# A two-layer block on one core: slots found by matmuls, biases gathered per slot, a reworked opening, and part of the first pass in seven products

## The chip, the core and the metric

The kernel runs on one core of a Trainium2 chip. A core has TensorE (PE), VectorE (DVE), ScalarE (ACT), GpSimd (POOL) and SyncE (SP), which run their own instruction streams and meet at semaphores, and 16 DMA engines. The metric is the device time of one execution in microseconds. The kernel before takes 2854.79 us, the median of three runs (2854.2 to 2859.41).

## The reference

There are 8 x 256 = 2048 tokens of 512 channels, all in float32. The block has two layers, each of the form x + attention(norm(x)) + ffn(norm(x)).

```python
xn = _layernorm(x)
x = x + _L0_attn_ref(xn, ...) + _L0_ffn_ref(xn, ...)
xn = _layernorm(x)
x = x + _L1_attn_ref(xn, ...) + _L1_ffn_ref(xn, ...)
```

Layer 0's attention is a linear attention with 32 heads of 128: q, k, v (with silu) and a gate (sigmoid), each a projection of 512 channels to 4096; scores times a decay instead of a softmax; a root-mean-square norm over all heads; gate times result through an output projection of 4096 to 512. Layer 0's feed-forward is a mixture of 16 experts with two chosen per token, plus a shared expert:

```python
scores = softmax(xt @ router_w + router_b) + router_bias
# keep the best 2 of 4 groups, then the best 2 experts of those
y += ge[:, None] * ((silu(xt @ w1 + b1) * (xt @ w2 + b2)) @ w3 + b3)   # each expert
z = (silu(xt @ sw1 + sb1) * (xt @ sw2 + sb2)) @ sw3 + sb3              # shared
```

Note that the expert's output bias b3 is inside the bracket that the gate multiplies. Layer 1 is one softmax attention head of 128 and a feed-forward of 64 low-rank adapters of rank 16, with 16 chosen per token.

## The kernel before

**Tiling.** Tokens are handled in four chunks of 512 (`NCH`), each of four tiles of 128 (`TPC`). The kernel has four stages.

**1. The opening** (lines 140 to 525). Per chunk: `normalize` (226) on DVE with a root on ACT; `turn_rows` (240), four PE transposes per tile into a bank and one copy out; `token_sums` (369), sums and differences of token blocks on POOL, stored to DRAM (`xc`) for the later passes; `shared_up` (317), the shared expert's up projections, 16 matmuls of 512 columns; `route` (265), router matmuls of 16 columns and then the choice on DVE; `decays` (357), exponentials on ACT; `clear` (410), zeros written over `xd`, a DRAM buffer of 47 x 128 slots; and, one chunk late, `share` (347), which calls `shared_down` (329). That one transposes the gates (L333), copies them, and for each token tile multiplies the 17 gates into the 17 rows of biases (L338) ahead of the shared expert's two products (L340). All expert biases are thus added per token. `first_two` (250) chooses two of n by comparing all pairs, n x n elements a token. Router weights, gates, choices and masks lie in the pool `work1`, whose memory the next stage takes over.

After the last chunk follows the dispatch (447 to 523): two matmuls of counts (L482 to L484), and a chain of small DVE steps that yields, for each token and each of its two choices, a slot in 47 tiles of 128 slots (`slots`, `slot_gates`), each tile owned by one expert (`rows_`).

**2. Attention of layer 0** (599 to 1215), the bulk. It goes over the chunks (pass i), in each over 8 groups of 4 heads (g), in each over the seven products p1 to p7 of a Strassen scheme in Winograd's form (`ORDER` = p1, p2, p6, p5, p3, p7, p4), and each of these is a product of blocks that is itself done in smaller blocks, of 128 channels. An `Outer` (960) is one such step. In passes 2 to 4 the inner blocks too are done in seven products (`p1`, `p7`, `p6`, `p4`, `p2`, `p5` and, inside the following step, `p3`; 1037 to 1066). In the first pass `plain` (981) does them in eight. `product` (661) is four matmuls of 128 columns. `weights` (605) loads a step's four weight blocks; for p6, p5, p3 and p7 it makes them as sums of loaded blocks on DVE (`outer_sum`), and for all makes the four inner sums on POOL (`inner_sum`), which in the first pass only go to DRAM (`ws`) for the later passes. The steps p1, p2 and p4 (`RAW`) have weights that are loaded as they are. Weights lie in a ring of three buffers.

The order of work is written by hand: after each product `slot` (679) takes due pieces from a list that `later(after, f)` (675) fills, "after" being a number of slots; ACT and POOL keep program order here (`manual_schedule`, 599), while the other engines' instructions are ordered by the framework's planner. In SP's queue the DMAs wait in order.

Among the pieces are the experts. In the first pass `row` (1086) loads a tile of normalized tokens from `xnd` and `scatter` (1093) writes its rows to their slots in `xd`, twice, by an indirect DMA on POOL. From the second pass on `Expert` (689) takes the tiles of slots one by one: the tokens from `xd` by SP, the weights by an indirect DMA on POOL, `turn` at 8 slots, `up` at 11, `down` at 14, whose result ACT copies (L733) and SP stores in `yd`. At a pass's end `load_sum` (933) loads the chunk's running sum (`xr`), and `finish` (586) adds the attention to it on DVE.

**3. The hand-over** (`wrapped_up`, 1145): the first chunk's expert results are gathered by slot from `yd` (`gather`, `settle`) and normalized in one piece, with the last steps of attention running.

**4. Layer 1** (1258 on): per chunk a `Head` (routing on 64 columns, q and k on 512, values, softmax) interleaved with the low-rank products in seven. `next_x` (1289) loads the next chunk's sum.

Of the kernel before, what the change touches and what calls it, by code (L numbers as in the profile page):

```python
# [9 lines left out]
FP = mybir.dt.float32  # L10
I32 = mybir.dt.int32
# [6 lines left out]
NT = B * S  # L18
P = 128
# [28 lines left out]
NEVER = -3.0e38  # L48

# [17 lines left out]
def block_kernel(  # L67
# [75 lines left out]
    def once(shape, name):  # L143
        return work.tile(shape, FP, tag=name, name=name, bufs=1)

    scratch = big("scratch").rearrange("p (h b) n -> p h (b n)", h=4)
    xs = [work.tile([P, TPC, C], FP, tag="x", name=f"x{i}", bufs=NCH) for i in range(NCH)]
    x_t = x.rearrange("(i t p) c -> i t p c", t=TPC, p=P)
    for t in range(TPC):
        nc.sync.dma_start(out=xs[0][:, t, :], in_=x_t[0, t])  # L150
# [8 lines left out]
    nc.sync.dma_start(out=wsh, in_=w_sh)  # L159
# [5 lines left out]
    b3_t = held[0 : E + 1, SH * C : (SH + 1) * C]  # L165
    nc.sync.dma_start(out=b3_t, in_=b3)
# [8 lines left out]
    xd = dram.tile([NSLOT, C], FP, name="xd")  # L175
# [7 lines left out]
    xnd = [dram.tile([P, TPC, C], FP, name=f"xnd{i}") for i in range(NCH)]  # L183
# [5 lines left out]
    zero = held[:, (SH + 1) * C : (SH + 2) * C].unsqueeze(1)  # L189
    nc.gpsimd.memset(zero, 0.0)  # L190

    ident = const.tile([P, P], FP, name="ident")
    make_identity(nc, ident)
    eps_t = const.tile([P, 1], FP, name="eps_t")
    nc.gpsimd.memset(eps_t, EPS)
# [5 lines left out]
    before = once([P, E, E], "before")  # L201
# [8 lines left out]
    dist = const.tile([P, S + P], FP, name="dist")  # L210
# [15 lines left out]
    def normalize(o, xc):  # L226

        mv = small.tile([P, TPC, 2], FP, tag="mv", name="mv")
        for t in range(TPC):
            st = small.tile([P, 6], FP, tag="st", name="st")  # L230
            nc.vector.bn_stats(st, xc[:, t, :])
            nc.vector.bn_aggr(mv[:, t, :], st)
        rstd = small.tile([P, TPC], FP, tag="rstd", name="rstd")
        rsqrt(rstd, mv[:, :, 1])
        for t in range(TPC):
            nc.vector.tensor_scalar(
                o[:, t, :], xc[:, t, :], mv[:, t, 0:1], rstd[:, t : t + 1], ALU.subtract, ALU.mult
            )

    def turn_rows(xT, xn, t, pt):  # L240
# [4 lines left out]
        if t % 2:  # L245
            nc.scalar.copy(o, i)
        else:
            nc.vector.tensor_copy(o, i)

# [15 lines left out]
    def route(xT, ge, sel):  # L265

        full = [P, TPC, E]
        pl = ps_sc()
        for t in range(TPC):
            for c in range(NC):  # L270
                mm(
# [57 lines left out]
    def shared_down(i, hT):  # L329
        xc = xs[i]  # L330
        pg = ps_sc()
        for t in range(TPC):
            nc.tensor.transpose(pg[0 : E + 1, bass.ts(t, P)], gates[i][:, t, :], ident)  # L333
# [1288 lines left out]
```

## Time and profile before

| | |
|---|---|
| median of the runs | 2854.79 us |
| the profiled execution, its own time | 2856.16 us |
| its span, first to last instruction | 2854.4 us |
| first projection matmul of the attention (L666) | 164.4 us |
| first matmul of the first p6 step | 186.7 us |
| last matmul of the attention (L878) | about 2551.6 us |
| PE busy / DVE / ACT / POOL | 2796.7 / 1569.7 / 948.2 / 1465.7 us |
| DMA | 763.21 MB, mean 267 GB/s |
| PE idle in passes 2 to 4, 800 to 2550, by releaser | DVE r 7.7, DVE mv 2.6, POOL gT 1.8, others under 1.4 each |

A float32 matmul stands in the trace as two entries (and two weight loads), a transpose as one. The mean length of an entry is longer than what it costs, because entries overlap: what counts is the distance from one start to the next. On a fast clock that is 0.112 us for 128 columns, 0.216 for 256 and 0.43 for 512. POOL's sums of 128x512 take 1.27 us each; an indirect DMA takes POOL 1.0 us to issue, and lands 7.5 us later for the experts' weights (1.3 MB), 7.3 for the scatters and 6.2 for the gathers of 256 KB from `yd` (medians).

### The profile page before, as it was taken

The numbers are of one execution on the slowest core, as the hardware profiler recorded it, in microseconds if no ns is written. First come the engines' busy times: TensorE is split into PE (matmuls) and PEld (weight loads), VectorE is DVE, ScalarE is ACT, GpSimd is POOL, SyncE is SP. The second block draws the span as 40 slices with busy tenths as digits, with TensorE's granted clock in tenths as the row PEclk, the third lists the DMA queues.
The fourth block names the chain that finished last, engine by engine and source line by source line (L and its number), as shares of the span: only waits on it lengthen the run. The fifth ranks groups of instructions, "written<-read, shape, count | busy, mean of one in ns | idle before, by whom it ended". The sixth has DMA issues, their size and how long they took to land. (4 is left out here: it accounts for less than half of the span.)

```text
span 2854.4 us, 49572 instructions
## 1 busy us (share of the span) xinstructions
PE 2796.7 (98%) x19864; PEld 2566.1 (90%) x19864; DVE 1569.7 (55%) x2615; ACT 948.2 (33%) x1683; POOL 1465.7 (51%) x1213
## 2 busy tenths in 40 slices
PE   8989999999999999999999999999999999999999
PEld 4469999999999999999999999999999999987877
DVE  6555666666654445444545555555555555556663
ACT  3312222212244333333443333443444333432221
POOL 4545666665546555555645454545544566552210
PEclk9999999999999999999999999999999999999999
DMA  7888998899986777778877777777777788652211
GB/s 255 301 309 337 357 352 341 341 349 347 364 320 246 262 266 273 282 270 299 296 265 257 264 266 265 259 274 280 284 259 259 267 310 298 222 212 88 76 61 61
DMA packets 161943, 763.21 MB, mean 267 GB/s; under 512 B 18209, under 2 KB 24225, under 8 KB 109874
## 3 DMA queue, kind: packets, MB, share of 16 engines
q1 hardware_dynamic: 149826, 706.25, 66.9%
q0 software_dynamic: 11888, 53.79, 5.2%
q8 instruction: 157, 2.57, 0.4%
q14 instruction: 72, 0.59, 0.1%
HBM read 596.14 MB, written 163.05 MB: 266 GB/s over the span
## 5 line engine op out<-in xcount | busy, mean ns | idle before, releaser
L666 PE MATMUL ps_a<-xt,w 128*128 128x128 f32 x5376 | 750.9, 276 | 11.7 <-DVE r L97 7.7
L666 PEld LDWEIGHTS ps_a<-xt,w 128*128 128x128 f32 x5376 | 681.9, 192 | 30.1 <-issue 14.3
L97 POOL TENSOR_TENSOR c<-c 128x512 f32<-128x512 f32 x216 | 271.7, 1273 | 262.0 <-DVE c L97 259.9
L97 POOL TENSOR_TENSOR c<-c,r 128x512 f32<-128x512 f32 x240 | 318.4, 1347 | 158.9 <-DVE r L97 153.1
L666 PE MATMUL ps_e<-xt,w 128*128 128x128 f32 x2688 | 373.4, 275 | 1.3 <-DVE c L97 1.3
L97 POOL TENSOR_TENSOR sums<-sums,sq 128x512 f32<-128x512 f32 x120 | 153.3, 1278 | 426.4 <-ACT sq L796 425.6
L996 ACT COPY cp<-ps_a 128x512 f32<-128x512 f32 x336 | 196.4, 585 | 476.0 <-PE ps_a L666 468.8
L666 PEld LDWEIGHTS ps_e<-xt,w 128*128 128x128 f32 x2688 | 344.4, 192 | 11.2 <-issue 3.8
L97 POOL TENSOR_TENSOR w<-w 128x512 f32<-128x512 f32 x224 | 294.6, 1325 | 108.2 <-issue 31.2
L666 PE MATMUL ps_a<-w,xt 128*128 128x128 f32 x1792 | 346.7, 275 | 0.0
L858 PE MATMUL ps_sc<-wo,gT 128*128 128x256 f32 x1288 | 305.1, 379 | 1.8 <-POOL gT L97 1.8
L97 DVE TENSOR_TENSOR acc<-ps_sc,acc 128x512 f32<-128x512 f32 x208 | 143.3, 690 | 265.8 <-PE ps_sc L858 198.8
L666 PEld LDWEIGHTS ps_a<-w,xt 128*128 128x128 f32 x1792 | 272.3, 192 | 0.0
L97 DVE TENSOR_TENSOR c<-ps_a,c 128x512 f32<-128x512 f32 x232 | 157.9, 686 | 202.7 <-PE ps_a L666 201.7
L858 PEld LDWEIGHTS ps_sc<-wo,gT 128*128 128x128 f32 x1288 | 232.3, 190 | 26.8 <-POOL gT L97 2.0
L666 PE MATMUL ps_b<-xt,w 128*128 128x128 f32 x1680 | 236.4, 277 | 6.8 <-ACT c L1010 4.2
L801 DVE SCALAR_TENSOR_TENSOR gT<-ps_o,nw,c 128x256 f32<-128x256 f32 x256 | 112.0, 479 | 231.0 <-ACT sq L796 222.0
L666 PEld LDWEIGHTS ps_b<-xt,w 128*128 128x128 f32 x1680 | 217.3, 194 | 17.5 <-issue 8.2
L744 ACT ACTIVATE c<-c 128x512 f32<-128x512 f32 x256 | 148.9, 627 | 170.1 <-DVE c L97 170.0
L796 ACT ACTIVATE sq<-ps_o 128x512 f32<-128x512 f32 x120 | 71.6, 597 | 382.3 <-PE ps_o L782 382.3
L666 PE MATMUL ps_e<-w,xt 128*128 128x128 f32 x896 | 173.2, 275 | 0.0
L97 DVE TENSOR_TENSOR s<-ps_sc,decay 128x384 f32<-128x384 f32 x256 | 139.8, 552 | 40.7 <-PE ps_sc L770 38.1
(299 smaller groups left out, 4635.8 us busy)
## 6 DMA issues: line engine op xcount, KB each, us to landing
w<-in_w_att_dram SPq DMA_DIRECT2D x128, 1024.0 KB
st<-in_w_att_dram SPq DMA_DIRECT2D x32, 1024.0 KB
wo<-in_w_out_dram SPq DMA_DIRECT2D x113, 256.0 KB
decay<-dec SPq DMA_DIRECT2D x64, 384.0 KB
w<-ws0p SPq DMA_DIRECT2D x12, 1792.0 KB
w<-ws1p SPq DMA_DIRECT2D x12, 1792.0 KB
w<-ws2p SPq DMA_DIRECT2D x12, 1792.0 KB
w<-ws3p SPq DMA_DIRECT2D x12, 1792.0 KB
```

The lines of the kernel that those rows point to most:

```text
L97: (eng or nc.vector).tensor_tensor(o, a, b, op)
L666: mm(bank[:, bass.ts(ty, P)], a, b, start=(first and ty == 0), stop=True, skip_group_check=True,)
L744: nc.scalar.activation(qk, qk, AF.Silu)
L796: nc.scalar.activation(sq, po, AF.Square)
L801: nc.vector.scalar_tensor_tensor(gT[:, h, :].rearrange("p (t n) -> p t n", t=2), po[:, bass.ts(h, S)].rearrange("p (t n) -> p t n", t=2), ...
L858: mm(py[:, bass.ts(t, S)], self.O[p][:, hh, bass.ts(t, P)], self.wo[p][:, hh, :], start=(t == 0 and hh == 0), stop=(hh == 1), skip_group_c ...
L996: nc.scalar.copy(c, bank)
```

## The change

- **Tokens.** `xd`, `clear`, `row` and `scatter` go. `find(g)`, once in each group of the first pass, makes for four (choice, tile) pairs a 128x128 matrix of ones where a token's slot has this partition, and a 128x47 one with the token's number where the slot has this tile, and adds up their products on PE: `whose` then holds, for each slot, its token. `Expert` gathers its tokens from `xnd` by an indirect DMA on POOL, next to that of the weights.
- **Biases.** No gates are transposed and no bias matmul stands in `shared_down`. `Expert.bias` gathers for each slot the owner's row of b3 into the token buffer, by a third indirect DMA on POOL at 12 slots, and `down`, now at 18, adds it on DVE in place of ACT's copy. `turn` is at 10, `up` at 13. The shared expert's own bias is broadcast and added by four POOL sums per chunk (`last_bias`).
- **Opening.** Half of the first chunk's tiles are loaded from ACT's queue, and the shared weights too; ACT's root is used once early; 16 transposes of the identity (`WARM`) run on PE ahead of the first data; the first chunk is normalized tile by tile; a chunk's transposes come right after the previous chunk's routing; router matmuls stand between the up projections. `chosen_two` chooses two of 16 with DVE's eight maxima and a replacement; `first_two` stays for the four groups. Gates, choices and masks move from `work1` to the `acc` tile.
- **First pass.** Steps with p in `RAW` (p1, p2, p4) are done in seven inner products in the first pass too; their inner sums, of weights and of tokens, are used on PE at once. The order of the inner sums changes, with 7 first.
- **Hand-over and layer 1.** The first normalization of layer 1 is cut into pieces of the list; the first `Head` interleaves q and k with the routing (`opening`).

```diff
-        nc.sync.dma_start(out=xs[0][:, t, :], in_=x_t[0, t])
+        (nc.scalar if t % 2 else nc.sync).dma_start(out=xs[0][:, t, :], in_=x_t[0, t])
...
+    nc.scalar.activation(root[:, 0:1], eps_t, AF.Sqrt)
+    nc.scalar.dma_start(out=wsh, in_=w_sh)
...
+    idle = ps_o()
+    for n in range(WARM):
+        nc.tensor.transpose(idle[:, bass.ts(n % 4, P)], ident, ident)
...
+    def chosen_two(keep, v):
+        top = scratch[:, 0, 0 : TPC * 8].rearrange("p (t n) -> p t n", t=TPC)
+        rest = scratch[:, 0, TPC * 8 : TPC * (8 + E)].rearrange("p (t n) -> p t n", t=TPC)
+        for t in range(TPC):
+            nc.vector.max(top[:, t, :], v[:, t, :])
+        nc.vector.tensor_copy(pair[:, :, 0:2], top[:, :, 0:2])
+        for t in range(TPC):
+            nc.vector.match_replace(rest[:, t, :], pair[:, t, :], v[:, t, :], -NEVER)
+        nc.vector.tensor_scalar(keep, rest, -NEVER, None, ALU.is_equal)
...
             project(p1, wsh, e, i)
+            between()
             project(p2, wsh, SH + e, i)
+            between()
...
-        gT = work.tile([E + 1, CH], FP, tag="geT", name="geT", bufs=1)
-        nc.scalar.copy(gT, pg[0 : E + 1, :])
         for t in range(TPC):
             py = ps_mm()
-            mm(py, gT[:, bass.ts(t, P)], b3_t, start=True, stop=False)
...
+        pl, tiles = ps_sc(), list(range(TPC))
+        ups.append(shared_up(i, lambda: scores(pl, xT[i], tiles.pop(0))))
+        ge = disp.tile([P, TPC, E], FP, name=f"ge{i}")
+        route(pl, ge, sel_all[:, bass.ts(i, TPC), :])
         gates.append(ge)
+        if i + 1 < NCH:
+            turn(i + 1)
         decays(i)
-        clear(i)
...
+    def last_bias(r, t3):
+        nc.sync.dma_start(out=t3, in_=b3[E : E + 1].to_broadcast([P, C]))
+        for t in range(TPC):
+            add(r[:, t, :], r[:, t, :], t3, nc.gpsimd)
...
-                    if o == 7:
+                    if o == 6:
                         nc.sync.dma_start(out=ws[g][p], in_=w[:, 4 if p in RAW else 1 : 8])
...
+                if p in RAW:
+                    return sums_of(w)
...
+        for t in first_sums:
+            sub(t[:, 4], t[:, 1], t[:, 0], nc.gpsimd)
+            sub(t[:, 1], t[:, 3], t[:, 1], nc.gpsimd)
+            sub(t[:, 5], t[:, 3], t[:, 4], nc.gpsimd)
+            sub(t[:, 6], t[:, 2], t[:, 5], nc.gpsimd)
...
-                nc.sync.dma_start(out=self.xe, in_=xd[bass.ts(j, P), :])
+                nc.gpsimd.indirect_dma_start(
+                    out=self.xe, out_offset=None, in_=xnd[:, :],
+                    in_offset=bass.IndirectOffsetOnAxis(ap=whose[:, j : j + 1], axis=0),
...
+            def bias(self):
+                nc.gpsimd.indirect_dma_start(
+                    out=self.xe, out_offset=None, in_=b3[:, :],
+                    in_offset=bass.IndirectOffsetOnAxis(ap=own_[:, self.j : self.j + 1], axis=0),
...
-                nc.scalar.copy(ye, py)
+                add(ye, py, self.xe)
...
             def go(self, bank, p, first=False):
                 product(bank, self.w[p], self.x[p], first)
                 slot()
+                if self.following:
+                    self.following.step()
...
-            later(8, e.turn)
-            later(11, e.up)
-            later(14, e.down)
+            later(10, e.turn)
+            later(12, e.bias)
+            later(13, e.up)
+            later(18, e.down)
...
+        def find(g):
...
+            for n in range(4):
+                at = 4 * g + n
+                nc.vector.tensor_scalar(ones_[:, n], count_, at_[:, 0, at : at + 1], None, ALU.is_equal)
+                nc.vector.tensor_scalar(
+                    theirs[:, n], count_[:, 0:NMT], at_[:, 1, at : at + 1],
+                    token[:, at % NTT : at % NTT + 1], ALU.is_equal, ALU.mult,
+                )
+            def add_up():
+                pt = ps_sc()
+                for n in range(4):
+                    mm(pt[:, 0:NMT], ones_[:, n], theirs[:, n], start=(n == 0), stop=(n == 3))
...
+            later(3, add_up)
...
+        def sevenfold(n):
+            return plan[n][0] > 0 or plan[n][2] in RAW
...
-            if i == 0:
+            last = outers[n - 1] if n and sevenfold(n - 1) else None
+            if not sevenfold(n):
+                if last:
+                    last.p3()
                 prepare(n + 2)
                 cur.plain(outers[n + 1])
                 continue
+            if i == 0:
+                while cur.steps:
+                    cur.step()
+                cur.following = outers[n + 1]
...
+        def opening(self):
+            self.pf = ps_sc()
...
+                for c in range(NC):
+                    mm(pm, wqkv_t[:, c, bass.ts(n, P)], self.yT[:, c, :], start=(c == 0), stop=(c == NC - 1))
+                    if c % 2:
+                        self.ranks(2 * n + c // 2)
+                nc.scalar.activation(o, pm, AF.Identity, bias=bqk_t[:, n : n + 1])
+            self.choose()
```

## The prediction

> **What bounds the kernel now.** I read the page's busy table and its 40 slices first, then the answer by stages, then the order of time on PE in the opening, then the costliest groups.
>
> ```profile
> PE 2796.7 (98%) x19864; PEld 2566.1 (90%) x19864; DVE 1569.7 (55%) x2615; ACT 948.2 (33%) x1683; POOL 1465.7 (51%) x1213
> ...
> PEclk9999999999999999999999999999999999999999
> DMA  7888998899986777778877777777777788652211
> ```
>
> PE has 57.7 us without work in 2854.4; nothing else is near full. So two things count: matmuls taken off PE, and the places where PE waits or runs slowly. The stages (columns PE, PEld, DVE, ACT, POOL, clock, DMA share) show where those are:
>
> ```profile
> 0.00:50.00 50.00, 38.79 (x133) 25.35 (x134) 33.40 (x81) 18.17 (x26) 20.70 (x40) 0.93 0.79 283
> 50.00:100.00 50.00, 46.20 (x144) 23.06 (x142) 29.04 (x52) 21.93 (x34) 28.24 (x38) 0.93 0.64 241
> 100.00:164.40 64.40, 59.23 (x166) 25.19 (x165) 33.88 (x69) 12.99 (x21) 33.00 (x52) 0.95 0.81 305
> 164.40:200.00 35.60, 27.39 (x217) 26.51 (x216) 24.02 (x55) 6.84 (x11) 7.24 (x6) 0.95 0.85 313
> 200.00:500.00 300.00, 296.99 (x2286) 286.53 (x2285) 179.17 (x283) 66.45 (x115) 181.97 (x144) 0.99 0.90 346
> ...
> 1600.00:2380.00 780.00, 775.26 (x5924) 739.71 (x5923) 402.30 (x603) 306.90 (x547) 414.05 (x320) 1.00 0.75 270
> ```
>
> The opening (to 164.4) and the 35 us behind it hold half of PE's idle time, at a clock below 1. From 200 on PE is full; there only less work helps. Inside the opening, in order of time (start, length, what; eight 512-column entries take 3.44 us from start to start when fast):
>
> ```profile
> 76.97 3.48 PE L271 MATMUL ps_sc<-rw,xT 128*128 128x16 f32 x16 [1.15 <-DVE xT L248]
> 80.28 5.50 PE L312 MATMUL ps_b<-xT,wsh 128*128 128x512 f32 x8
> 85.61 3.60 PE L312 MATMUL ps_a<-xT,wsh 128*128 128x512 f32 x8
> ...
> 97.62 0.60 PE L333 MATMUL ps_sc<-ident,ge 128*17 128x128 f32 x4
> 98.88 1.12 PE L338 MATMUL ps_b<-held,geT 17*128 17x512 f32 x2 [0.66 <-ACT geT L335]
> ...
> 101.85 1.12 PE L338 MATMUL ps_a<-held,geT 17*128 17x512 f32 x2
> ...
> 147.41 0.61 PE L333 MATMUL ps_sc<-ident,ge 128*17 128x128 f32 x4 [3.58 <-DVE ge L97]
> ```
>
> After a run of thin router matmuls (16 columns) the next wide ones run at 0.67 us instead of 0.43; and a down tile with its bias takes 2.97 us (98.88 to 101.85). Behind the opening, the first projections fill their banks, and the copy that would empty them waits for the dispatch:
>
> ```profile
> 175.33 0.58 ACT L1010 COPY c<-ps_b 128x512 f32<-128x512 f32 x1 [26.64 <-DVE disp L97]
> ```
>
> **What the Trainium skill says.** "TensorE: Matmul & The Clock Gate", section "What's actually happening": the array runs at half rate until a window of about 3.4 us was busy, and falls back after an idle one. The trace agrees on the factor: 512-column entries 0.855 us apart at 18.6 to 22.2, then 0.43. The same page, "Part 4: PE-mode transpose", says that transposes don't count as busy in this sense. The trace fits: 16 transposes and 24 router entries from 10.2 to 18.6 left the array slow. So I give the sixteen WARM transposes nothing. "DMA: Bandwidth & Descriptors", "Anatomy of one DMA — SWDGE (gpsimd) path", gives 2.0 us plus bytes by 436e3; for a 256 KB gather that would be 2.6 us (estimate). The trace has 6.2 us for the same size (yd into spare), which I use. "GPSIMD Engine Reference", "Key points": GpSimd cannot read PSUM and shares SBUF interfaces with VectorE. The trace shows its 128x512 sums at 1.26 us, up to 1.79 when VectorE is active.
>
> **The change, part by part.** The sum is against the profiled execution (2856.2 us, span 2854.4); its median is 2854.8, 1.4 less.
>
> *Opening to the first projection (164.4 now).* PE's floor, in entries of the trace (two per float32 matmul, one per transpose): 128 up-projection and 64 down entries at 0.43 (82.6), 32 bias entries with their switch 20.0, 128 router entries at 0.107 (13.7), 64 + 16 transposes at 0.11 (8.8), dispatch 1.2: 126.2. The other 38.2 are 10.2 before the first transpose, 10.0 of waits (64.4 + 100 less 144.2 busy, less 10.2), and 18.0 of slow clock.
> - Expert biases leave: a tile goes from 2.97 to 4 x 0.43 = 1.72, so 16 x 1.25 = 20.0; gate transposes 1.8 more. Floor 104.4.
> - Start: the first tile arrives by 3.5; statistics, root, reciprocal, scaling (0.69 + 0.18 + 0.25 + 0.17 + 0.54) and hand-overs are about 2 us per tile, so transposes run from 6.5 and the first wide product starts at about 12.8 instead of 18.6, since the scores no longer stand ahead of it. Half the x issues go to ACT, and w_sh waits there behind two small steps; its 1 MB still lands before 12.
> - Scores between wide products: no thin stretch cools the array. I keep 3 us of slow clock, at the start.
> - Choice by maxima: the 16x16 comparison costs VectorE 11.2 + 6.4 + 5.8 + 4.8 + 2.8 = 31.0 us in four chunks. Four maxima, a copy, four replacements and a compare: about 2.5 us a chunk by layer 1's rows (0.17; 0.08 + 0.21). It is hidden except at the end, where PE waited 3.58.
> - clear (12.3 MB) leaves SP and the DMA engines, some 32 us at the 380 GB/s of the full slices, so the token-sum stores go out sooner. VectorE has some 18 us a chunk beside PE's 26, POOL 18 to 22.
> - Waits: as low as 2, as high as 18 if POOL's token sums (60 us, with waits up to 15.7 for their own stores) become the pace; I take 8.
> Sum: 12.8 + 104.4 - 1.8 (the first transposes, ahead of 12.8) + 3 + 8 = 126.4, so **-38**.
>
> *To the start of p6 (186.7 now).* Two plain steps of 8 products x 8 entries x 0.1117 = 7.15 take 22.3 us with their stalls. In sevens they are 12.5. Gates and choices now lie in the acc tile, so copies and the decay load no longer wait for the dispatch. p6's blocks were issued at 175.55, behind that decay load, and used 11.2 later; now they can be issued with the weights, 1.2 after the opening, plus some 2 for sharing: 14.4. p6's weights become what is late. **-8** (-9.8 to 0).
>
> *Rest of the first pass.* The words say all in sevens; the code does so for p1, p2, p4 alone: 22 further steps x 8 entries x 0.1117 = 19.7 off PE. find adds 32 matmuls of 47 columns, 64 entries x 0.107 = 6.9 (VectorE about 1.5 a group, hidden). Net -12.8. POOL loses 32 scatters (1.0 each) with their waits and gains six 1.27 us adds a group. But sums that only fed a store now feed PE: four of 1.3 us after a load. In group 3, p4's load landed at 451.7 and its sums end at 457, with p4 starting at 453.5: by a hair. I charge 6 (0 to 23): **-7**.
>
> *Passes 2 to 4.* ye by VectorE instead of ACT: 47 x 0.69, hidden. POOL issues 94 gathers more at 1.0 and the token load leaves SP: POOL goes from 55% to 61% beside a full PE. The bias gather waits for the transposes two slots before; behind it on POOL stand result adds and gT differences; with 6.2 us against six slots (about 8 us) it lands in time. If late, VectorE stands at the expert's add, and PE behind its banks. last_bias makes POOL wait for 1 MB plus a broadcast on SP's queue and then add for 5.1 us, three times, with sums, p7 and p5 behind; their products are 6 to 7 slots later. **+3** (0 to 12).
>
> *Layer 1.* Statistics in pieces remove a stall of 2.57 and the slow clock after it (1.4); opening() replaces 5.15 + 8.7 us by 3.5 + 6.9. That is -7.4; the last chunk's bias adds (four of 1.27 on POOL between load and finish, partly under the spread loads that VectorE awaits) give back 2 (0 to 8). **-5**.
>
> Total -38 - 8 - 7 + 3 - 5 = -55: 2801 profiled, **2800** as a median.
>
> **The rivals.**
> - *Sums before PE (slower).* Loads in the first pass land as the step begins, as p4's did. Then the third sum ends 3.9 us into the step, after two products of 0.9: 2.1 us of wait, plus about 1.7 of slow clock. It decides from 2.8 us a step (60.8 / 22). With 3.8: 84 - 61 = +23, 2878. For: DMA at 0.90 there, three weight buffers, SP in order. Against: p1 and p2 had sums early or just in time; row loads and scatters (12.6 MB) are gone.
> - *Opening held by POOL or DMA.* Only -20 there and -4 behind it: -33, 2822. For: POOL's waits for xsum stores. Against: clear is gone.
> - *POOL late in later passes.* Of 94 us more issue time, 15% on PE: +14 more, 2814. Against: PE waited for POOL 1.8 us in all.
> - *Everything fits.* Opening -48 with p6, first pass -12.8, later 0, layer 1 -8: about -70, 2785.
>
> **How the numbers follow.** Forecast 0.57, opening held 0.18, POOL late 0.10, all fits 0.07, sums before PE 0.08. A difference under 0.2% (5.7 us) can't be told from none. Only the sums end slower (0.07, 0.01 level); POOL's tail adds 0.01 level: faster 0.91, same 0.02, slower 0.07. The range takes in the bounds, the held opening and the best case: 2776 to 2836; left out are the slower case and tails, under 0.2.
>
> **What would show it.** Right: first projection near 126; no 17-row matmuls; p6 by 142; 3392 instead of 3584 entries of L666 in the first pass; PE's waits in passes 2 to 4 still about 10 us. Wrong: PE waiting for POOL's w at p1 or p4, wide entries at 0.67 again in the opening, or waits for gT or ye behind POOL.

## The result, and the profile after

The kernel after takes 2821.22 us, the median of four runs (2818.98 to 2823.11), the kernel before in the same comparison 2857.1 (2854.2 to 2861.48): a ratio of 0.9873, 95% interval 0.9856 to 0.989. That is some 36 us less, where 55 were forecast. The sign and the range (2776 to 2836) held; the size did not. The total alone would point to the wrong rival: "opening held" was put at 2822, and the opening gained more than was forecast.

The page of the kernel after, busy time by engine and the two rows of slices:

```profile
PE 2757.3 (98%) x19704; PEld 2545.9 (90%) x19704; DVE 1671.7 (59%) x2795; ACT 948.8 (34%) x1683; POOL 1608.2 (57%) x1352
...
PEclk9999999999999999999999999999999999999999
DMA  7888888889877777777877777787877787552211
```

PE has 39 us less work; VectorE has 102 us more and POOL 143 more. PE's share is 98% as before, so the page doesn't show where the missing gain is. The stages do. I cut both traces at the same events: the first projection, then the matmuls with ones that end each pass. The answer by stages for the kernel after (length, then busy time of PE, PEld, DVE, ACT, POOL, then clock, DMA share, GB/s):

```profile
0.00:116.60 116.60, 110.62 (x406) 63.50 (x407) 79.40 (x234) 50.26 (x78) 76.69 (x142) 0.99 0.81 303
116.60:745.90 629.30, 612.25 (x4674) 586.46 (x4672) 462.57 (x715) 170.01 (x294) 398.97 (x304) 0.99 0.87 325
745.90:1364.80 618.90, 607.89 (x4605) 576.38 (x4605) 324.86 (x491) 228.19 (x409) 396.00 (x321) 0.99 0.77 284
1364.80:1957.60 592.80, 585.54 (x4465) 557.95 (x4464) 316.60 (x470) 225.39 (x402) 339.68 (x276) 1.00 0.75 273
1957.60:2511.20 553.60, 547.64 (x4151) 522.04 (x4151) 306.80 (x460) 217.26 (x383) 327.71 (x255) 1.00 0.73 269
2511.20:2820.10 308.90, 293.42 (x1411) 239.60 (x1409) 181.48 (x427) 57.67 (x117) 69.17 (x56) 0.98 0.24 83
```

| stage | before | after | change | forecast |
|---|---|---|---|---|
| opening | 164.4 | 116.6 | -47.8 | -38 |
| first pass | 633.8 | 629.3 | -4.5 | -15 (-8 to p6, -7 behind it) |
| pass 2 | 607.8 | 618.9 | +11.1 | |
| pass 3 | 587.8 | 592.8 | +5.0 | |
| pass 4 with the hand-over | 557.8 | 553.6 | -4.2 | |
| passes 2 to 4 | 1753.4 | 1765.3 | +11.9 | +3 |
| layer 1 | 302.8 | 308.9 | +6.1 | -5, hand-over included |

How far such a stage can be trusted: each figure is from the one profiled execution of its run. Between the kernel before and the tenth run below, which is the same code from pass 2 on, passes 2 to 4 agree to 0.2 us. In runs whose edits don't touch them, the opening lies between 116.6 and 120.5, pass 2 between 617.7 and 618.9, pass 3 between 592.8 and 593.9, pass 4 between 553.3 and 555.8 and layer 1 between 306.5 and 310.2. The first pass lies between 624.7 and 629.3 but for the sixth run (631.0) and the seventh (636.5), told below.

To the end of the first pass the forecast was right to 1 us (-52.3 for -53), but by luck: the opening gave 10 us more than forecast and the first pass 10.5 less. All of the missing 20 us lie behind it: stages that were to give 2 us took 18.

The opening, in order of time on PE, answers to the lines shown of before:

```profile
11.21 3.25 PE L306 MATMUL ps_sc<-rw,xT 128*128 128x16 f32 x24
14.31 3.68 PE L350 MATMUL ps_b<-xT,wsh 128*128 128x512 f32 x8
...
77.70 1.88 PE L374 MATMUL ps_b<-held,scratch 128*128 128x512 f32 x4
79.42 1.88 PE L374 MATMUL ps_a<-held,scratch 128*128 128x512 f32 x4
```

The first wide product is fast from its start, no 17-row matmul is left, a down tile takes 1.72 us from start to start, and no thin stretch slows what follows. The copy that stood 26.64 us idle, and the product behind it:

```profile
123.94 0.59 ACT L1085 COPY cp<-ps_a 128x512 f32<-128x512 f32 x1 [20.90 <-DVE disp L567]
...
124.58 1.40 PE L732 MATMUL ps_a<-xt,w 128*128 128x128 f32 x6 [4.15 <-ACT cp L1085]
```

The wait is still there, 4.15 us on PE (4.20 before). The first p6 step starts at 134.5 instead of 186.7: two steps in sevens are 14 products, and the fifteenth is under way at 136.57, the second of a pair on one bank that began right behind the sums of weights:

```profile
129.80 4.30 DVE L99 TENSOR_TENSOR w<-w,st 128x512 f32<-128x512 f32 x7
...
134.49 0.92 PE L732 MATMUL ps_a<-xt,w 128*128 128x128 f32 x6
```

From the first projection to p6 that is 17.9 us, 22.3 before.

### The profile page after: what moved, and what is told of

Same layout as the page of the kernel before. It is cut to its first block, busy times and chain, and to the rows that moved or that the text cites. A ratio compares the mean times of both kernels' runs of the same rounds, so it can differ in the third digit from the quotient of the medians.

```text
span 2820.1 us, 49618 instructions
## 1 busy us (share of the span) xinstructions
PE 2757.3 (98%) x19704; PEld 2545.9 (90%) x19704; DVE 1671.7 (59%) x2795; ACT 948.8 (34%) x1683; POOL 1608.2 (57%) x1352
## 4 chain that ended last, share of the span: by engine, by line
PE 79%; DVE 8%; DMA 5%; issue 4%; POOL 3%; ACT 1%; SPq 0%; DVEq 0%; POOLq 0%; ACTq 0%
PE ps_a L732 23%; PE ps_e L732 11%; PE ps_sc L943 9%; PE ps_b L732 6%; PE ps_o L866 4%; PE ps_sc L963 3%; PE ps_sc L854 3%; PE ps_sc L801 3%; PE ps_o L867 2%; PE ps_a L1655 2%; PE ps_sc L855 2%; DVE r L99 1%; DMA w<-in_w_att_dram 1%; PE ps_sc L813 1%; POOL w L99 1%
## 5 line engine op out<-in xcount | busy, mean ns | idle before, releaser
L99 POOL TENSOR_TENSOR c<-c 128x512 f32<-128x512 f32 x240 | 302.0, 1273 | 276.5 <-DVE c L99 260.7
L99 POOL TENSOR_TENSOR c<-c,r 128x512 f32<-128x512 f32 x264 | 347.5, 1337 | 176.4 <-DVE r L99 174.0
L1085 ACT COPY cp<-ps_a 128x512 f32<-128x512 f32 x384 | 224.3, 585 | 602.6 <-PE ps_a L732 578.7
L99 DVE TENSOR_TENSOR c<-ps_a,c 128x512 f32<-128x512 f32 x216 | 146.9, 687 | 141.5 <-PE ps_a L732 138.5
L732 PE MATMUL ps_b<-xt,w 128*128 128x128 f32 x1536 | 214.3, 275 | 1.8 <-DVE c L99 1.0
L732 PEld LDWEIGHTS ps_b<-xt,w 128*128 128x128 f32 x1536 | 195.2, 192 | 9.1 <-issue 6.1
```

Source lines behind the costliest of these rows:

```text
L99: (eng or nc.vector).tensor_tensor(o, a, b, op)
L732: mm(bank[:, bass.ts(ty, P)], a, b, start=(first and ty == 0), stop=True, skip_group_check=True,)
L1085: nc.scalar.copy(c, bank)
```

## Where the later time comes from, by the trace

**Pass 2.** PE waits for the turned tokens of an expert, seven times, once a group, 9.0 us in all. The order of time ahead of one such wait, kernel after:

```profile
934.61 2.94 POOL L99 TENSOR_TENSOR c<-c,r 128x512 f32<-128x512 f32 x2
934.63 3.46 DVE L99 TENSOR_TENSOR c<-c,r 128x512 f32<-128x512 f32 x2
...
937.51 1.71 POOL L99 TENSOR_TENSOR wo<-wo 128x512 f32<-128x512 f32 x1
938.02 0.68 DVE L785 COPY xeT<-ps_sc 128x512 f32<-128x512 f32 x1
...
938.75 1.49 PE L801 MATMUL ps_sc<-xeT,xw 128*128 128x128 f32 x11 [1.28 <-DVE xeT L785]
```

By the copies it is the second of a group's three experts (the expectation of run 1 calls it the third). The transposes end at about 934, but VectorE has just begun two sums of p7, 3.46 us, and the copy stands behind them. In the kernel before, at the same place of the group, the transposes stood two slots earlier, and the copy came ahead of the sum:

```profile
982.21 0.67 DVE L708 COPY xeT<-ps_sc 128x512 f32<-128x512 f32 x1
982.81 1.38 DVE L97 TENSOR_TENSOR c<-c,r 128x512 f32<-128x512 f32 x1
```

**The ends of passes 1 and 2.** At the end of pass 2 POOL waits for the row of the shared bias and adds it; then the chain to PE. After, then before:

```profile
1344.62 4.96 POOL L99 TENSOR_TENSOR spare<-spare,sb 128x512 f32<-128x512 f32 x4 [8.37 <-DMA sb<-in_b_dram]
...
1365.70 9.42 POOL L99 TENSOR_TENSOR acc<-acc 128x512 f32<-128x512 f32 x7
...
1372.27 4.73 DVE L644 SCALAR_TENSOR_TENSOR spare<-acc,rms,spare 128x512 f32<-128x512 f32 x4 [3.29 <-POOL acc L99]
...
1378.12 1.65 PE L732 MATMUL ps_e<-xt,w 128*128 128x128 f32 x6 [4.05 <-DVE c L99]
```

```profile
1403.22 9.43 POOL L97 TENSOR_TENSOR acc<-acc 128x512 f32<-128x512 f32 x7
...
1405.96 1.84 PE L946 MATMUL ps_sc<-ones,sums 128*128 128x1 f32 x16
...
1410.22 4.30 DVE L592 SCALAR_TENSOR_TENSOR spare<-acc,rms,spare 128x512 f32<-128x512 f32 x4
```

Before, POOL's seven sums began 2.7 us ahead of the matmuls with ones; after, they begin 0.9 us behind them (1364.80). VectorE waits for them, and PE's banks wait for VectorE.

At the end of the first pass the same row holds POOL, the gather of an expert's bias is issued late, and VectorE stands at the expert's add; POOL's next gather waits for that add, POOL's sums for the gather, and VectorE and PE for these:

```profile
745.02 0.69 DVE L99 TENSOR_TENSOR ye<-ps_sc,xw 128x512 f32<-128x512 f32 x1 [5.95 <-DMA xw<-in_b_dram,own__1086]
...
750.37 1.65 PE L732 MATMUL ps_a<-xt,w 128*128 128x128 f32 x6 [1.60 <-DVE r L99]
```

**Layer 1.** For the last chunk the adds stand ahead of the sum with the attention (`finish`). After, then before:

```profile
2687.84 5.82 POOL L99 TENSOR_TENSOR x<-x,sb 128x512 f32<-128x512 f32 x4 [20.68 <-DMA x<-xr]
2689.14 5.74 DVE L644 SCALAR_TENSOR_TENSOR x<-acc,rms,x 128x512 f32<-128x512 f32 x4 [2.79 <-POOL x L99]
...
2696.14 3.78 PE L1577 MATMUL ps_e<-t,fa 128*128 128x256 f32 x8 [5.20 <-DVE cp L99]
```

```profile
2728.32 2.74 DVE L592 SCALAR_TENSOR_TENSOR x<-acc,rms,x 128x512 f32<-128x512 f32 x4 [1.91 <-DMA x<-xr]
...
2732.84 1.99 PE L1434 MATMUL ps_e<-t,fa 128*128 128x256 f32 x8 [1.85 <-DVE cp L97]
```

The sum starts later and takes 5.74 instead of 2.74 us, PE waits 5.20 instead of 1.85, and then runs at half speed (3.78 for 1.99).

## The experiments

My theory after this reading: the loss is the order of single pieces (the expert's turn, the shared bias), not the amount of work. The rival: VectorE and POOL simply carry too much now. Totals of different runs often overlap in their intervals, so most verdicts below rest on the stage that the edit touches. Where runs 2, 3 and 10 leave out a bias, they are trials for timing only, since they compute something else.

**1. The expert's pieces two slots earlier.**

```diff
-            later(10, e.turn)
-            later(12, e.bias)
-            later(13, e.up)
+            later(8, e.turn)
+            later(10, e.bias)
+            later(11, e.up)
```

> The changed kernel with the expert's transposes, bias gather and up-projection two slots earlier (8, 10, 11 instead of 10, 12, 13; the down product stays at 18). Theory 'order of the pieces': in pass 2 the third expert of each group is turned just after VectorE was given the p7 results and their two sums, so the copy of the turned tokens stands behind 3.5 to 5 us of VectorE work and PE waits 1.28 us, seven times. Two slots earlier it stands before them: pass 2 falls from 618.9 to about 610 us, PE's waits for xeT from 9.0 to below 2, the other stages stay within 1.5 us; total about 2812. Rival 'more work on VectorE and POOL' (the result add that was on ScalarE, the gathers): waits for xeT stay near 9 wherever the piece stands, total 2821.

Measured: 2834.29 us, ratio 0.9923 (0.991 to 0.9937), slower than the kernel after; pass 2 627.1. PE's waits in pass 2:

```profile
PE ps_sc L783 <- DMA xw<-xnd,whose: 14.1, 6, 3.7
PE ps_a L732 <- DVE r L99: 3.5, 8, 1.6
```

The wait for the copy is gone, as the order of pieces said, but the transposes now meet a token gather that hasn't landed. So `turn` cannot go back to 8: its two slots pay for the gather that replaced SP's load. My total was wrong.

**2. Less work on VectorE and POOL, the same slots.** `bias` is not called, and the add is ScalarE's copy again:

```diff
-            later(12, e.bias)
...
-                add(ye, py, self.xe)
+                nc.scalar.copy(ye, py)
```

> The changed kernel without the gather of an expert's output bias and with ScalarE copying the down product, as before the change (the experts' output biases are left out); the slots of the pieces stay at 10, 13 and 18. 'Order of the pieces': PE's waits for xeT in pass 2 stay at 7 to 9 us and pass 2 stays above 616. 'More work on VectorE and POOL': the waits go, pass 2 falls to about 609.

Measured: 2820.6 us, 0.9875 (0.9859 to 0.989). VectorE has 17 us less to do in pass 2 and POOL 26, and the waits do not move:

```profile
PE ps_sc L801 <- DVE xeT L785: 9.0, 7, 1.3
```

Pass 2 is 614.8, under my bound of 616: the 4 us are its first group, where the gathered bias came late (745.02 above) and PE then ran at half speed, not these waits. The work isn't the cause of the 9 us.

**3. No shared bias.** Both calls of `last_bias` go.

```diff
-                    last_bias(self.r, attn.tile([P, C], FP, tag="sum", name="sb3", bufs=3))
...
-            last_bias(x_, work.tile([P, C], FP, tag="sb3", name="sb3", bufs=1))
```

> The changed kernel without the adds of the shared experts' output bias, and without its load, in all four chunks (that bias is left out). Theory 'the shared bias holds up POOL and VectorE': at the end of pass 2 POOL waits 8.4 us for the bias row and adds for 5.0, so its seven sums of acc start 3.6 us late, VectorE waits 3.3 us for them and PE 4.05; in layer 1 the last chunk's adds stand ahead of the rms sum of VectorE, which takes 5.7 instead of 2.7 us and starts later, and PE waits 5.2 us and then runs slowly. Without it pass 3 falls from 592.8 to about 588.5, pass 4 by 0 to 2, layer 1 from 308.9 to about 302; total about 2809. Rival 'two gathers more per expert hold up POOL at the pass's end': pass 3 stays at 592 or more. Rival 'layer 1 lost it in the reworked opening': layer 1 stays at 308.

Measured: 2805.02 us, 0.982 (0.9805 to 0.9835). Pass 3 589.1 (-3.7), pass 4 553.6 (no gain), layer 1 301.6 (-7.3), and pass 2 613.3 (-5.6), of which I had expected nothing. The theory holds; both rivals, the gathers at the pass's end and the opening of layer 1, fall.

**4. The shared bias later.** The load and the adds come six slots after the load of `r`; in layer 1, after `finish`:

```diff
-                    last_bias(self.r, attn.tile([P, C], FP, tag="sum", name="sb3", bufs=3))
+                    later(6, self.load_bias)
...
-            last_bias(x_, work.tile([P, C], FP, tag="sb3", name="sb3", bufs=1))
             finish(i, x_)
+            last_bias(x_, work.tile([P, C], FP, tag="sb3", name="sb3", bufs=1))
```

> The changed kernel with the same adds of the shared bias, placed otherwise: in the passes the bias row is loaded and added six slots (about 9.5 us) after the load of the 1 MB that it is added to, and for the last chunk in layer 1 the adds come after VectorE's rms sum instead of before it. If the wait of 8.4 us on POOL is what costs, it gives nearly all that leaving the adds out gives: pass 3 about 589, layer 1 about 302.5, total about 2810. If the 5 us of adding costs, pass 3 stays at 592 to 593 and only layer 1 gains.

Measured: 2812.1 us, 0.9847 (0.9832 to 0.9862): pass 2 614.6, pass 3 591.3, pass 4 555.8 (the edit doesn't reach it), layer 1 305.9. In pass 2 it gives 4.3 of the 5.6 us that leaving the adds out gives, in pass 3 1.5 of 3.7, in layer 1 3.0 of 7.3. The waits say more than these lengths. In pass 3 PE's wait of 4.05 us falls to 2.3 (1.7 in run 3), so there the place is most of it; most of what remains is a stretch of 3.4 us at half clock that run 3 doesn't have. In layer 1 PE's wait for `cp` is still 4.7 us (5.2 without the edit), and the 3.0 us are about what fewer stretches at half clock are worth. So neither answer is whole: at the end of a pass the place costs, in layer 1 the adds cost at both places tried. There `finish` now comes first and yet takes 4.75 us; the adds of the first tiles run beside its last ones.

**5. Only the up-projection later.**

```diff
-            later(13, e.up)
+            later(15, e.up)
```

> The changed kernel with the expert's up-projection two slots later (15 instead of 13); its transposes, both gathers and its down product stay where they are. The first trial moved the transposes and ran into the token gather, which had not landed. Theory 'order of the pieces' (the copy of the turned tokens stands behind VectorE's sums of p7, and the up-projection follows it three slots on): PE's waits of 1.28 us for xeT leave pass 2, which falls from 618.9 to 610, total about 2812. Rival: the up-projection is only moved closer to the down product (two to three slots), and the wait turns up there as a wait for he, or the slot it moves to delays another piece by as much: pass 2 stays above 616, total 2819 to 2823.

Measured: 2811.27 us, 0.9837 (0.9812 to 0.9862). Pass 2 is 607.4 (-11.5), what it was before the change, and the up-projection starts without a wait:

```profile
750.76 0.94 PE L732 MATMUL ps_a<-xt,w 128*128 128x128 f32 x6 [2.12 <-DVE r L99]
...
932.20 0.68 DVE L785 COPY xeT<-ps_sc 128x512 f32<-128x512 f32 x1
...
933.92 1.95 PE L801 MATMUL ps_sc<-xeT,xw 128*128 128x128 f32 x16
```

With runs 1 and 2 this settles the 9 us: one number in a list of slots. The other 2.5 us aren't shown to be the edit's: the stall at the start of the pass is still there (750.76), but PE didn't run at half speed behind it, as it did in the kernel after.

**6. The shared bias in the opening.** POOL adds the row to each tile of x right after its token sums, and nowhere else:

```diff
         token_sums(i)
+        for t in range(TPC):
+            add(xs[i][:, t, :], xs[i][:, t, :], sb3, nc.gpsimd)
```

> The changed kernel with the shared bias added in the opening instead (POOL adds the row to each tile of x after its token sums, 16 adds of 1.27 us, 20 us in all), and no such adds in the passes and in layer 1. Theory 'the adds cost by their place': pass 2 first group, pass 3 and layer 1 give what leaving the adds out gave (613, 589, 301.6), and the opening stays within 2 us, as POOL is busy for 77 of 117 us there: total about 2806. Rival 'POOL paces the opening': its token sums and the adds end later than VectorE needs the tiles, and the opening grows by 5 to 15 us: total 2812 to 2822.

Measured: 2822.47 us, 0.9868 (0.984 to 0.9896). The later stages give about what was expected (614.1, 589.1, 303.9), but the opening takes 131.2. Not by POOL's sum, as the rival had it, but by its order:

```profile
12.38 1.26 POOL L99 TENSOR_TENSOR x<-x,held 128x512 f32<-128x512 f32 x1 [9.89 <-DMA held<-in_b_dram]
...
17.77 3.60 PE L308 MATMUL ps_sc<-rw,xT 128*128 128x16 f32 x16 [5.21 <-ACT xT L276]
```

POOL waits 9.89 us for the bias row, the distances behind it are late, ScalarE waits for them with its decays, the copy of the transposed tokens stands behind these, and PE waits 5.21 us and then runs slowly.

**7. No WARM.** `WARM = 0`.

> The changed kernel without the 16 transposes of WARM. The prediction gave them nothing. If that holds, the opening stays at 116.6 to 120.5 us, with the first wide products at the same pace with or without them. Rival 'they warm the array': the first wide product starts at about 14.3 with entries at 0.86 instead of 0.43 us, until about 18 to 22, and the opening grows by 2 to 4 us.

Measured: 2827.61 us, 0.9889 (0.9861 to 0.9917); the opening is 117.6, within its scatter. The last of the first transposes, the router products and the first wide product:

```profile
10.82 0.74 PE L271 MATMUL ps_a<-ident,xn 128*128 128x128 f32 x4
11.40 2.75 PE L306 MATMUL ps_sc<-rw,xT 128*128 128x16 f32 x24
14.00 5.38 PE L350 MATMUL ps_b<-xT,wsh 128*128 128x512 f32 x8
```

The first eight wide entries take 5.38 us instead of 3.68, which looks like the rival. But the other runs have the transposes, and in runs 1 to 4 these entries take 5.38 to 5.78 us all the same. Run 3:

```profile
14.32 5.38 PE L350 MATMUL ps_b<-xT,wsh 128*128 128x512 f32 x8
```

The clock on record shows why. It changes between half and full in steps of about 3.4 us, whose offset differs from one execution to the next. In the kernel after it was full from 5.4, half again from 8.8 and full from 12.2 on: what WARM had brought was gone before the product at 14.3. In run 3 the same changes came at 5.2, 8.6 and 12.0, and it was half once more from 15.4 to 18.8. In runs 1, 2 and 4 it became full only behind 20. So the pace of that product can't be laid to WARM; what WARM is worth stays open. The scatter of the opening is mostly this: runs 1, 2 and 4 have 120.4 to 120.5.

The first pass was 636.5 in this run. PE waited for gT up to 3.0 us at a time, and stretches at half clock add up to 17.1 us there, against 6.8 in the kernel after; by half of the difference, 5 us, they account for most of the excess (an estimate). No part of the edit reaches there.

**8. The first pass plain again.** p1, p2 and p4 in eight products, without their token sums.

```diff
-            return plan[n][0] > 0 or plan[n][2] in RAW
+            return plan[n][0] > 0
```

> The changed kernel with all of the first pass plain, as before the change: p1, p2 and p4 in eight products instead of seven, and no token sums ahead of the first step. My step gave the sevens 2.7 us of the first two steps and 19.7 us of the other 22, less 6 for sums that now feed PE. If that holds, the first pass grows from 629.3 by 14 to 20 us, total 2835 to 2841. Rival 'the sums eat the gain': the first pass grows by under 6 us.

Measured: 2819.91 us, 0.9866 (0.9837 to 0.9894), and the first pass 628.4: the sevens gain nothing. The first pass of this kernel:

```profile
114.50:742.90 628.40, 623.04 (x4847) 601.76 (x4846) 418.21 (x691) 141.08 (x242) 332.43 (x256) 1.00 0.86 327
```

Against the line of the kernel after: 173 entries more, 19.3 us at 0.1117, but PE is busy only 10.8 us longer, and idle for 5.4 instead of 17.1 us. (Of the other 8.5 us, some 3.4 are the 6.8 us at half clock that this run doesn't have; the rest isn't broken down.) My rival for this run is right. Where the idle time is: the 4.15 us at the first copy, which a step in sevens needs after four products and a plain one only after eight; and gT (gate times attention, what the output projection multiplies), 3.5 instead of 7.8 us. Ahead of a wait for gT, kernel after:

```profile
336.94 1.28 DVE L1184 TENSOR_SCALAR ones__2907<-count__1091,at__1088 128x128 f32<-128x128 f32 x1 [2.48 <-POOL c L99]
...
338.17 1.24 DVE L1185 TENSOR_SCALAR theirs<-count__1091,at__1088,token 128x47 f32<-128x47 f32 x1
...
340.80 0.86 DVE L886 SCALAR_TENSOR_TENSOR gT<-ps_o,nw,c 128x256 f32<-128x256 f32 x2
341.32 1.99 PE L963 MATMUL ps_sc<-wo,gT 128*128 128x256 f32 x8 [2.05 <-DVE gT L886]
...
342.05 0.27 DVE L1184 TENSOR_SCALAR ones__2907<-count__1091,at__1088 128x128 f32<-128x128 f32 x1
```

Four of `find`'s eight small instructions stand ahead of gT. Beside POOL's sums they take 1.24 to 1.34 us; with POOL idle (342.05) 0.27.

**9. Two edits in the first pass.** The last chunk's residual is stored tile by tile; `find` is cut into four pieces (`mark`), three slots apart.

```diff
+            if i + 1 == NCH:
+                tc.keep_in_program_order(nc.sync.dma_start(out=xr[i][:, t, :], in_=xc[:, t, :]))
...
-            later(3, add_up)
+            for n in range(4):
+                later(3 * n, partial(mark, n))
+            later(12, add_up)
```

> The changed kernel with two edits in the first pass: the last chunk's residual is stored in four tiles as each is ready, not in one store of 1 MB, and each group's finding of tokens is given to VectorE in four pieces, three slots apart, instead of eight instructions in a row. Theory 'the sevens were worth their 19 us, and stalls beside them took it': the copy that waits 4.15 us behind the first products is held by the landing of that store, and the gates gT wait behind the eight small instructions, which take 1.25 us each instead of 0.28 while POOL adds. Then the first wait falls by 2 to 4 us with the slow clock behind it, PE's waits for gT fall from 7.8 to below 3, and the first pass from 629.3 to 615 to 621. Rival 'VectorE and POOL are simply too full beside the sevens': the waits turn up elsewhere on VectorE's results and the first pass stays above 625.

Measured: 2814.99 us, 0.9856 (0.9832 to 0.988); the first pass 621.5, at the upper end of what was expected, and below all the untouched ones (624.7 and more). The waits in it:

```profile
PE ps_sc L966 <- DVE gT L889: 3.4, 5, 1.4
PE ps_a L735 <- ACT cp L1088: 2.4, 1, 2.4
```

gT fell from 7.8 to 3.4 us (6.5 to 9.7 in the runs that leave the sevens and `find` alone), so cutting up `find` is what helped. The first copy fell from 4.15 to 2.4 us, but without this edit PE waited there from 2.0 to 4.1 us in runs 1 to 5 and 7, so that half of the edit isn't shown to help. With the stalls of gT mended the sevens are worth 628.4 - 621.5 = 6.9 of their 19.3 us, an upper value, since a plain first pass would gain from a cut-up `find` too.

**10. The kernel before, without the biases in the opening.** No gate transposes, and two products instead of three per down tile:

```diff
-            mm(py, gT[:, bass.ts(t, P)], b3_t, start=True, stop=False)
```

> The kernel before without the gate transposes and the product with the experts' biases in the opening (the biases of routed and shared experts are left out). My step took 20.0 us for the 16 tiles' bias entries with their switches and 1.8 us for the gate transposes. If that holds, the opening falls from 164.4 to 141 to 144. Rival 'VectorE's choice by comparison was the opening's pace': PE then waits for VectorE instead, and the opening stays above 150.

Measured: 2843.22 us, 0.9953 (0.9944 to 0.9963). The opening falls to 132.4, 32 us instead of my 21.8, since PE's waits for the gates (3.58 and 2.0) leave too, and 9 us at half clock, worth some 4.5 (an estimate; part of that is chance, as in run 7). But the kernel gains only 14.5, because the first pass starts against a wall:

```profile
163.34 0.59 ACT L1004 COPY c<-ps_b 128x512 f32<-128x512 f32 x1 [42.72 <-DMA xr<-x]
...
163.97 1.65 PE L660 MATMUL ps_b<-xt,w 128*128 128x128 f32 x6 [22.92 <-ACT c L1004]
```

By its releaser, ScalarE's copy waits for the store of the residual; my reading is that the store still reads memory that the opening gives back. That store stands in SP's queue behind stores of token sums that POOL hasn't made (they go out until 157.4). So taking matmuls off PE by itself was worth 13 of 32 us at the end of the first pass. The other half of the opening's gain needs what else the change does there: fewer stores on SP, the residual's place in its order, masks and gates out of that memory. Which of these carries it was not tried one by one.

**11 and 12. The causes mended together.** Both have the edits of runs 5 and 9. Run 11 puts the shared bias in the opening, but in POOL's order behind each chunk's sums; run 12 does so for the last chunk alone, and for the others adds it six slots after the load, as run 4. In the opening's loop, run 11, then run 12:

```diff
         decays(i)
+        for n in ((0,), (1,), (2, 3), ())[i]:
+            for t in range(TPC):
+                tc.keep_in_program_order(
+                    nc.gpsimd.tensor_tensor(xs[n][:, t, :], xs[n][:, t, :], sb3, ALU.add)
+                )
```

```diff
         decays(i)
+        if i == 2:
+            for t in range(TPC):
+                tc.keep_in_program_order(
+                    nc.gpsimd.tensor_tensor(xs[3][:, t, :], xs[3][:, t, :], sb3, ALU.add)
+                )
```

> The changed kernel with both edits of the first pass, the up-projection two slots later, and the shared bias added in the opening, on POOL after each chunk's token sums and decays, where it cannot stand before the distances that the decays need (the first trial in the opening made ScalarE and the transposes wait for the bias row). If the causes add up: first pass about 618, pass 2 about 603, pass 3 589, layer 1 302, opening 117 to 121, total 2782 to 2792. If POOL's 20 us more pace the opening again, it is 125 or more and the total is near 2795 to 2800.

> As the kernel with all mended, but the shared bias is added in the opening for the last chunk alone (4 POOL adds, 5 us) and in the passes six slots after the load for the other three. In the kernel with all 16 adds in the opening the opening took 125.4 us instead of 116.7. If POOL's adds in the opening cost by their sum, four cost about 2: opening about 119, first pass 620 to 622, pass 2 604 to 606, pass 3 591, pass 4 556, layer 1 302, total 2792 to 2796. If they cost by standing in POOL's order at all, or if the first pass only shifts by what the opening gives, it is 2798 to 2803.

Measured: 2801.11 us, 0.9805 (0.9782 to 0.9828), and 2799.8 us, 0.9801 (0.9782 to 0.9821). By stages: opening 125.4 and 119.0, first pass 624.9 and 621.2, pass 2 604.3 and 606.4, pass 3 590.4 and 591.0, pass 4 554.6 and 556.8, layer 1 301.9 and 299.3. Run 11 missed its 2782 to 2792 by its opening and the first pass behind it. Run 12 met its stages (layer 1 came 3 us below), with 2795.44 in the profiled run; its median of 2799.8 lies in the band that was given to the rival. Both intervals lie wholly below that of the change as made. They beat both kernels and can't be told from each other.

## Why the prediction was right in sign, and where its size failed

- *Opening, -38, measured -47.8.* The terms held in the trace: first wide product at 14.3 with 24 of the router entries already done (12.8 forecast), 1.72 us a tile. Better than said were the slow clock (none behind 14.3 for 3 us forecast) and the waits behind it (97.0 less 95.4 busy, 20 to 117: 1.6 for 8). Of this some 4 us are luck: in runs 1, 2 and 4, the same code there, the first wide product came at half clock and the opening was 120.4 to 120.5. WARM was given nothing, and nothing more is shown. The reason given for it, from the skill page "TensorE: Matmul & The Clock Gate", "Part 4: PE-mode transpose", that transposes don't count as busy, was not borne out: in run 7 PE did nothing but transposes from 8.24, and from 11.2 on they followed each other at 0.11 instead of 0.21 us. Run 10 adds that the bias entries alone would not have given the gain.
- *To p6, -8, measured -4.4* (17.9 us for 22.3). That p6 starts 52.2 us earlier in all, for 46, is the opening's doing. p6's weights didn't become what is late, but a wait of 4.15 us stayed, although the gates had left `work1`. The step "copies and the decay load no longer wait for the dispatch" failed in part: the first copy came 7.3 us into the pass instead of 10.9. In runs 9 to 11 the trace names the residual's store as what this copy waits for; for the kernel after it names VectorE, and that it is the store there too is argued from its place in SP's queue, not shown.
- *Rest of the first pass, -7, measured -0.1.* The term "19.7 off PE" is about right as a count (173 entries fewer in the whole pass, run 8) and wrong as time: run 8 shows no gain at all. The charge of 6 was laid to sums that feed PE; PE waited 0.9 us for those. What took the gain was VectorE: gT behind `find`, which I had called hidden (run 9). "Sums before PE (slower)" didn't happen.
- *Passes 2 to 4, +3 (0 to 12), measured +11.9 with the hand-over's 4 inside it.* This is the step that failed. PE was to wait about 10 us there still; it waits 24.6 (14.5 before). The terms counted POOL's issue time and the shared bias; the retiming of `turn`, `up` and `down` was given no cost. It costs 9.0 us of waits (runs 1, 2 and 5). That the bias gather "lands in time" failed: VectorE stood waiting for it five times, 13.4 us in all, but only at 745, behind the shared bias, did PE pay for it. "Products are 6 to 7 slots later" was about the wrong reader: the adds delay POOL's seven sums, which VectorE and then PE await, 4.05 us. The rival "POOL late" had nearly the right time (2814), half by this mechanism; for the 9 us it is wrong, since less POOL work changed nothing.
- *Layer 1, -5, measured +6.1.* `opening()` took 10.5 us for 13.85, as forecast, but the gain is gone again by the second `Head`, which reaches its scores 88.3 us into the stage (87.9 before): 2.2 us come back as a wait of the gates' transposes, with half speed behind it. The hand-over's stall left, and that gain lies in pass 4. The mechanism of the last chunk was named and sized 2; it is 7.3 (run 3).

So 9.0 for the retiming, 5.6 and 3.7 at the ends of the first two passes (run 3), and 5.3 above the charge in layer 1: some 23.6 us, of which the forecast had charged 3, for the 20 that are missing. They aren't quite additive: run 5 alone brings pass 2 back to 607.4 with the shared bias still in place. And stretches at half clock, which come and go between executions, are in all of these figures: one of 6.8 us lies in pass 2 of the kernel after and in none of runs 2 to 6 and 8.

## What to carry to other kernels

In a list of timed pieces, moving a producer by two slots can put it behind another engine's burst: print the order before and after, and look at what each moved piece now stands behind, and what stands behind it. An add that costs 5 us of an idle engine is free only where nobody queues on that engine: ask which sum of it is awaited first, and place the add behind that. And fewer matmuls on a full PE are worth only what the next engine lets through: the sevens here gave nothing until the small VectorE work beside them was cut up, and at most 6.9 us then. Last, before a pace at the start of a kernel is laid to a warm-up, look at the same instructions in several executions.

## What the runs showed of the hardware

- VectorE's time beside POOL's sums depended on where its operands lie. Results read from PSUM stayed at 0.68 to 0.69 us beside POOL's sums (the copy at 938.02). Sums of two SBUF tiles took 1.73 (3.46 for two) and the scaled sums of `finish` 1.4 instead of 0.69 (layer 1), and small instructions from SBUF alone 1.24 to 1.34 instead of 0.27. The skill page "GPSIMD Engine Reference", "Key points", names VectorE instructions with two SBUF inputs among those that contend; the trace agrees, and shows that the smallest instructions suffer most in proportion.
- The recorded clock changed between half and full in steps of about 3.4 us with another offset in each execution. With the same instructions ahead of it, the first wide product took 3.68 us in the kernel after and in runs 5, 8 and 9, and 5.38 to 5.78 in runs 1 to 4. Transposes alone brought the full clock (run 7, at 11.2).
- How long PE stalls doesn't tell whether half speed follows. In the kernel after, a stall of 1.6 us (750.37) cost about 4 us, since the entries behind it ran at half speed until 756; sixteen one-column products stood shortly before it. In run 5, at the same place and behind the same products, a stall of 2.12 us (750.76) cost no more than itself, and so did those of 1.28 us (938.75).
